# p of images 2 to 7 with three nested products and two reads by ScalarE, f by seven products for images 7 and 8, bias in column tiles

## The chip, the cores and the metric

The kernel runs on one core of one Trainium2 chip. The metric is the device time of one execution in microseconds. The engines are TensorE (PE, with its weight loads PEld), VectorE (DVE), ScalarE (ACT), GpSimd (POOL), and SyncE (SP), which issues most DMAs. All data are fp32.

## The reference, cut to what matters

The input x has 8 images of 512 channels and 32 x 32 = 1024 positions. Two layers follow each other:

```
q, k, v = Wq x + bq, Wk x + bk, Wv x + bv           # 8 heads of 64 channels
attn    = softmax(q^T k / 8)                        # per head, 1024 x 1024
x       = x + Wp (attn v) + bp                      # "p"
g, theta, phi = g_w x + g_b, theta_w x + theta_b, phi_w x + phi_b   # 256 channels each
f       = theta phi^T / 1024                        # 256 x 256
z       = W_w (f g) + W_b + x
out     = batch norm of z over images and positions
```

So every 1x1 convolution is a product of a weight matrix of 512 (or 256) x 512 with a matrix of 512 x 1024 per image. f is a product over the 1024 positions.

## The kernel before, in words

**Stages.** Images are counted 1 to 8 here, b = 0 to 7 in the code. For each image the kernel runs attention, then q, v and k of the next image, then p of this image (`project`), then theta and phi together (tensor ptp into tp, `theta_phi`), then f, g and the product of f with W_w (`nonlocal_`). TensorE works through one strict queue. A helper `pe` (and `dve` for some operations of VectorE and GpSimd) pins operations in the order of the program; where an operation isn't pinned, a scheduler places it. SP issues the loads of weights in the order of the program; a load waits until its buffer (a ring of four) is free.

**Products by seven.** A product of matrices cut into 2 x 2 blocks is done by seven products of half size in place of eight, with sums of blocks on both sides (`weight_sums`, `data_sums`/`more_sums`: t1 to t4 of the data). The table `SEVEN` lists them: name, weight block, data block, slot, and which quarters of the result the product goes to. A half-size product of p is four matmuls of 128x512. `nested` does the same again inside a half-size product: seven quarter-size products, each one matmul of 128x256, in place of four matmuls of 128x512. It needs inner sums of the weight block (`nest`, made once and kept in DRAM) and of the data block (`inner_sums`).

**The stage p.** For images 2 to 7 `seven` takes its products from `INNER["p"]`: five plain products (`FIVE`) and two nested ones. The third entry of `INNER["p"]`, read by `for _ in range(next(counts, 0)): next(steps)`, says how many nested steps follow each main matmul: none for the first four, then one after each. The results lie in PSUM in four slots of two banks each; tags[0] and tags[1] hold slots 0 and 1 of the main products, tags[2:] the nested ones. Main products in order: "11" (slot 0), s1t1 (slot 1), s2t2 (slot 0), s4 (slot 1), s3t3 (slot 0). After each product its result is added into quarters of x by VectorE: the first time with the bias bp (L773, two 128x512 operations), later by one 128x1024 operation (L471). The sums t1 and t2 of the new x, for the next stage, come after p; t3 and t4 in the next stage (L261).

**Before p.** In the stage k of the next image GpSimd makes the sums of o, the attention's output (`i_o` and `t_o`), and, at the end of `six`, two 128x1024 additions into k (`add("22", "T7")`, `add("21", "T7")`).

**f.** `make_f` is 16 matmuls of 128x256 and one copy by ScalarE; `seven_f` is 28 matmuls of 128x128 with sums on VectorE before (`f_sums`) and after. Images 1 to 6 use `seven_f`, images 7 and 8 `make_f`. f of image 7 is computed inside the attention of image 8 (`held_f`, at its step 2), f of image 8 within pg of its own `nonlocal_`.

**The bias.** At image 1 only, four products of one column (`bias_product`) add Wp bv to bp: TensorE into PSUM, a copy by ScalarE, an addition by VectorE, ahead of the products den that give the softmax denominators.

Of the kernel before, what the change touches and what calls it, by code (L numbers as in the profile page):

```python
# [8 lines left out]
F32 = mybir.dt.float32  # L9
# [7 lines left out]
P = 128  # L17
# [13 lines left out]
def unshifted(ctx: ExitStack, tc: tile.TileContext, a: dict, out: bass.AP):  # L31
# [79 lines left out]
    for b in range(1, B):  # L111
# [4 lines left out]
    PAIRS = ((1, 6), (3, 4), (5, 2))  # L116
    UNITS = {"WqT": PAIRS, "WkT": PAIRS, "WvT": PAIRS, "WpT": ((1, 2), (3, 4, 5), (6,)), "tp": ((1, 2), (3, 4, 5), (6,)),
             "WgT": (range(7),)}
# [41 lines left out]
    def fetch(w, n, t=None, dma=None):  # L160
        dma, name = dma or nc.sync, w.name
        if t is None:
            t = wf0.tile([P, 2 * w.half], F32, tag="w0", name=f"w0_{name}") if n == "first" else \
                wr.tile([P, WIDTH], F32, tag="w", name=f"w_{name}_{n}")
        blocks = w.place(n, t)
        if name in kept:
            of = kept["plain" if w.last else name][n]
            sp(dma.dma_start(w.whole(n) if w.last else w.tiles[n], of))
            return
        if n == 0:  # L170
            corner[name] = block(f"a21_{name}")[:, :, :w.half]
# [36 lines left out]
    def inner_weights(w, i):  # L208
# [3 lines left out]
                for to, l, r, op in ((s3, a11, a21, ALU.subtract), (a21, a21, a22, ALU.add), (s2, a21, a11, ALU.subtract),  # L212
                                     (s4, a12, s2, ALU.subtract))]

    def nest(w, i):
        for one in inner_weights(w, i):
            one()
# [10 lines left out]
    def join_bias(t):  # L228
# [6 lines left out]
        def more(c):  # L235
# [4 lines left out]
                15: more(1), 17: get(2, 1), 22: more(2), 25: get(3, 1), 30: more(3)}  # L240

    def bias_product(t, ps):
        for oc in range(CC):
            pe(nc.tensor.matmul(ps[:, oc:oc + 1], t[:, oc * P:(oc + 1) * P], ones, start=True, stop=True,
                                skip_group_check=True))
# [30 lines left out]
    def quarters_of(t):  # L276
# [50 lines left out]
    def seven(name, w, data, positions_out, first, add, between=None, early=False,  # L327
              by_chunk=False, inner=None):

# [19 lines left out]
        for n, (what, wi, di, s, reads) in enumerate(products):  # L349
# [14 lines left out]
            for i, (to_ps, at, lhsT, rhs, k) in enumerate(work):  # L364
# [11 lines left out]

    def six(name, w, data, positions_out, at, begin, third, fills, by_scalar=False):

# [78 lines left out]
        if by_scalar:  # L457
            add("T7", "T6")
        add("22", "T7")
        add("21", "T7")  # L460

# [40 lines left out]

    ones = const.tile([P, 1], F32, tag="ones", name="ones")
    nc.vector.memset(ones, 1.0)
    eps = const.tile([P, 1], F32, tag="eps", name="eps")
# [22 lines left out]
    def heads_of(b, what, w, bias, data, pin=lambda ins: None, steps=None, fills=None, **how):  # L528
# [3 lines left out]
        if fills is not None:  # L532
            def begin(to, ps, i):
                nc.scalar.activation(to, ps, AF.Identity, bias=bias[:, i:i + 1])
# [7 lines left out]
            six(f"p{what}_{b}", w, data, False, lambda q: t[:, rows(q), cols(q)], begin, third, fills,  # L542
                what == "q")
            return t
# [31 lines left out]
    def attention(b, q, k, v, near_end, make_f=None):  # L576
# [10 lines left out]
        rows = {}  # L587
        tags = list(free)

        def part(u):  # L590
# [92 lines left out]
        def all_denominators(ps):  # L683

            t = folded.pop("t")
            if b == 0:
                bias_product(t[:, 3, :], ps[:, 1, :CC])
            den = ps[:, 0, :256]
            in_tiles(den, [(folds4, t[:, 0, :])])
            ri = t[:, 2, :256]  # L690
            dve(nc.vector.reciprocal(ri, den))
# [73 lines left out]

    def project(b, xt, w, between, data):
        def first(q, ps):
            if isinstance(q[0], slice):
                ps = ps.unsqueeze(1)
            for m in range(ps.shape[1]):  # L770
# [3 lines left out]
                if b == B - 1 and q in ("11", "22"):  # L774
                    dve(ins)

        seven(f"pp_{b}", w, data, False, first, add_to(xt), between, early=b == B - 1 and "later",
              inner="p" if 0 < b < B - 1 else None)

# [87 lines left out]

    def make_f(b, tp, ps):
        f = block("f").rearrange("p a n -> p (a n)")[:, :IC * CI].rearrange("p (c d) -> p c d", c=IC)
        ps = ps[:, 0, :].rearrange("p (c d) -> p c d", c=IC)  # L870
        order = [*range(NB // 2, NB), *range(NB // 2)]
        for c in range(IC):
            for i in order:
                pe(nc.tensor.matmul(ps[:, c, :], tp[:, i, c * P:(c + 1) * P], tp[:, i, CI:],
                                    start=(i == order[0]), stop=(i == order[-1])))
        nc.scalar.mul(f, ps, 1.0 / N)
        return f

    def nonlocal_(b, xt, data, f, wg, before_wf, between=None, theta=None, tp=None):

        scaled = theta is None
        if theta:
            phi = f_sums(b, tp, CI)
            f = lambda ps: seven_f(theta, phi, ps)
        ww = block(f"ww_{b}")
# [10 lines left out]
        def first(q, ps):  # L896
# [3 lines left out]
            else:  # L900
# [3 lines left out]
              lambda q, ps: nc.vector.tensor_tensor(part(q), part(q), ps[:, 0, :], ALU.add),  # L904
              between or {4 if theta else 5: f_meanwhile}, early=bool(between))
        f = fs[0]
# [3 lines left out]
        for d in range(IC):  # L910
            ps = next_bank(f"pwf_{b}_{d}")[:, 0, :]
            for c in range(IC):
                pe(nc.tensor.matmul(ps, f[:, c, d * P:(d + 1) * P], ww[:, c, :], start=(c == 0), stop=(c == IC - 1)))  # L913
            nc.scalar.mul(wf[:, d, :], ps, 1.0 if scaled else 1.0 / N)
        if b >= B - LATE:
# [151 lines left out]
    for b in range(B):  # L1067
        last = b == B - 1
        nxt = {}
        if b == 1:  # L1070
            nest(w_tp, 1)
            nest(w_tp, 2)
            keep("tp", w_tp, (0,))
            load_w()
# [34 lines left out]
        def held_f(ps):  # L1109
            held["f"] = make_f(b - 1, held["tp"], ps)  # L1110

        o, denominators, normalize = attention(b, q, k, v, near_end, held_f if last else None)
        between = None
        if not last:
# [4 lines left out]
                (0, 0): t4[:1], (0, 3): t4[1:2], (0, 13): t4[2:3], (1, 0): t4[3:]})  # L1119
            products = normalize(denominators(next_bank(f"den_{b}")))  # L1120
            v = values(b + 1, weights("WvT"), data, fills={(1, 13): products})

# [4 lines left out]
            if b:  # L1127
                more = [lambda: inner_sums(nxt["o"], "t4", dve, nc.gpsimd)]
                o_sums = [lambda: inner_sums(nxt["o"], "21", dve, nc.gpsimd), *o_sums]
            else:  # L1130
                w_p = loaded[1]
                more = [lambda i=i: weight_sums(w_p, corner["WpT"], (i,), dve, nc.gpsimd) for i in (3, 4, 5)]
            k = heads_of(b + 1, "k", weights("WkT"), bk, data, dve, steps=dk, fills={
                (0, 13): [*o_sums, *(more if b else ())], (1, 13): () if b else more,
                (2, 0): () if b else [lambda: weight_sums(w_p, corner["WpT"], (6,), dve, nc.gpsimd)]})
        else:
# [17 lines left out]
        w = weights("WpT", sums_done=True)  # L1154
        project(b, xt, w, between, nxt["o"])
        if b == 0:
# [9 lines left out]
        data = data_sums(quarters_of(xt), f"x1_{b}", (1, 2, 3, 4) if last else (1, 2))  # L1166
        if last:
            reload_chunks(B - LATE)
        elif b > B - LATE and b != B - 2:
            z[b] = [xt[:, cc, :] for cc in range(CC)]  # L1170
# [25 lines left out]
        def before_wf():  # L1196
            if last:
# [3 lines left out]
                take_back(B - LATE + 1)  # L1201

        if last:
            take_back(B - LATE)
        if b == B - 2:
            held.update(x=xt, tp=tp)
        else:
            nonlocal_(b, xt, data, lambda ps: make_f(b, tp, ps), weights("WgT"), before_wf,
                      theta=of_theta[0] if of_theta else None, tp=tp)
            load_w()  # L1210
# [230 lines left out]
```

## Time and profile before

| What | us |
|---|---|
| Median of 3 runs (2103.86 to 2104.8) | 2104.62 |
| The profiled execution | 2104.33 |
| Its span | 2102.5 |
| Mean granted TensorE clock, share of full | 0.996 |

Groups of instructions that the change concerns (busy time in all and mean of one, then the idle time of the engine before them):

```profile
L365 PE MATMUL pp<-t_o,w_WpT 128*128 128x512 f32 x208 | 101.0, 592 | 0.0
L365 PE MATMUL pp<-o,w_WpT 128*128 128x512 f32 x144 | 67.7, 592 | 0.0
L773 DVE SCALAR_TENSOR_TENSOR x<-pp,bp,x 128x512 f32<-128x512 f32 x52 | 37.5, 746 | 33.0 <-PE pp L365 33.0
```

A matmul of the program on fp32 data appears as two records, so 208 and 144 records of pp stand for 176 matmuls (20 each for images 2 to 7, 28 each for images 1 and 8). The busy time of matmuls counts overlapping records once, while the mean of one includes the time until its result is written. In the timeline, a row merges neighbouring instructions of one kind: its start, its length, engine, line, operation, and how many; the bracket tells how long the engine was idle before and what ended that.

### The profile page before, as it was taken

The page shows a single profiled execution, that of the slowest core. Times are in us where ns is not written, and L with a number is a line of the kernel's source. Part 1 is how long each engine was busy: PE and PEld are TensorE (multiplying, and loading weights), DVE is VectorE, ACT ScalarE, POOL GpSimd, SP SyncE. Part 2 cuts the span into 40 slices and gives each one's busy share as a digit, 9 for nine tenths or more (in the row PEclk, how much of TensorE's full clock was granted, in tenths as well). Part 3 has the DMA queues.
Part 4 walks back from the last instruction along what each step waited for, and adds up shares of the span by engine and source line. Part 5 has one row for each costly group of instructions (what it writes and reads, how often), then busy time and mean ns, then how long its engine had stood idle before and what let it go on. Part 6 is the DMA issues. An engine that isn't in the chain of part 4 may idle for free.

```text
span 2102.5 us, 34141 instructions
## 1 busy us (share of the span) xinstructions
PE 2080.0 (99%) x13598; PEld 1170.5 (56%) x13598; DVE 1426.5 (68%) x2137; ACT 790.5 (38%) x1045; POOL 734.0 (35%) x637
## 2 busy tenths in 40 slices
PE   9999999999999999999999999999999999999995
PEld 4535864358733677336773377633875348733472
DVE  5587567875677656876567766677665775656746
ACT  1465204652046410464105631066312653056116
POOL 0024800348113581134812356123670338411010
PEclk9999999999999999999999999999999999999998
DMA  6254534345343443435324363153644345312768
GB/s 230 83 145 77 162 137 142 42 87 153 105 115 38 94 142 106 118 40 115 131 90 122 40 147 119 67 126 41 159 144 154 40 53 168 100 29 39 218 253 321
DMA packets 76727, 246.78 MB, mean 117 GB/s; under 512 B 16657, under 2 KB 25105, under 8 KB 74513
## 3 DMA queue, kind: packets, MB, share of 16 engines
q1 hardware_dynamic: 62688, 218.16, 31.8%
q0 software_dynamic: 12016, 24.80, 12.2%
q8 instruction: 109, 1.79, 0.4%
q10 hardware_dynamic: 1856, 1.56, 0.3%
q14 instruction: 58, 0.47, 0.1%
HBM read 163.20 MB, written 47.71 MB: 100 GB/s over the span
## 4 chain that ended last, share of the span: by engine, by line
PE 98%; ACT 1%; DVE 1%; DMA 0%; issue 0%; DVEq 0%
PE ps L602 21%; PE po L628 21%; PE pp L365 7%; PE ptp L365 7%; PE pv_in L441 6%; PE pk_in L444 6%; PE pq_in L444 6%; PE pg L365 5%; PE pz L365 3%; PE ptp_in_s L313 2%; PE pf L857 2%; PE pp_in_s L316 2%; PE pwf L913 1%; PE pv L408 1%; PE pq L411 1%; PE pq L365 1%
## 5 line engine op out<-in xcount | busy, mean ns | idle before, releaser
L605 ACT ACTIVATE e<-ps 128x1024 f32<-128x1024 f32 x512 | 523.0, 1025 | 422.2 <-PE ps L602 412.1
L658 POOL DMA_DIRECT2D fold<-acc x336 | 257.1, 816 | 949.2 <-DMA fold<-acc 637.4
L611 DVE TENSOR_TENSOR acc<-acc,e 128x1024 f32<-128x1024 f32 x384 | 469.9, 1224 | 103.1 <-ACT e L605 93.6
L602 PE MATMUL ps<-q,k 64*64 64x512 f32 x4096 | 529.4, 589 | 0.0
L628 PE MATMUL po<-e,v 64*64 64x512 f32 x4096 | 528.7, 589 | 0.0
L628 PEld LDWEIGHTS po<-e,v 64*64 64x64 f32 x4096 | 156.6, 133 | 282.9 <-issue 275.7
L602 PEld LDWEIGHTS ps<-q,k 64*64 64x64 f32 x4096 | 155.5, 133 | 283.4 <-issue 275.6
L901 ACT ACTIVATE g<-pg,gb 128x512 f32<-128x512 f32 x31 | 21.3, 688 | 436.3 <-PE pg L365 436.2
L609 DVE TENSOR_TENSOR acc<-e,e 128x1024 f32<-128x1024 f32 x64 | 78.3, 1224 | 118.2 <-ACT e L605 116.0
L365 PE MATMUL pp<-t_o,w_WpT 128*128 128x512 f32 x208 | 101.0, 592 | 0.0
L365 PE MATMUL ptp<-w_tp,t_x 128*128 128x256 f32 x400 | 96.1, 379 | 0.0
L720 POOL TENSOR_TENSOR o<-o,r 128x1024 f32<-128x1024 f32 x28 | 65.5, 2362 | 36.3 <-DMA r<-den_d 35.8
L365 PEld LDWEIGHTS ptp<-w_tp,t_x 128*128 128x128 f32 x400 | 72.3, 190 | 7.8
L452 DVE TENSOR_TENSOR k<-k,pk_in 128x256 f32<-128x256 f32 x112 | 46.8, 421 | 39.5 <-PE pk_in L444 35.0
L365 PE MATMUL ptp<-w_tp,x 128*128 128x256 f32 x272 | 69.6, 380 | 0.0
L365 PE MATMUL pp<-o,w_WpT 128*128 128x512 f32 x144 | 67.7, 592 | 0.0
L450 ACT COPY v<-pv_in 128x256 f32<-128x256 f32 x84 | 31.4, 374 | 95.8 <-DVE T_pv L452 25.5
L452 DVE TENSOR_TENSOR v<-v,pv_in 128x256 f32<-128x256 f32 x112 | 46.2, 421 | 29.6 <-PE pv_in L441 23.1
L450 ACT COPY k<-pk_in 128x256 f32<-128x256 f32 x84 | 31.3, 372 | 91.6 <-PE pk_in L444 89.9
L773 DVE SCALAR_TENSOR_TENSOR x<-pp,bp,x 128x512 f32<-128x512 f32 x52 | 37.5, 746 | 33.0 <-PE pp L365 33.0
L441 PE MATMUL pv_in<-w_WvT,i_t_x 128*128 128x128 f32 x448 | 59.2, 275 | 0.0
L444 PE MATMUL pk_in<-i_t_x,w_WkT 128*128 128x256 f32 x224 | 57.8, 381 | 0.0
(249 smaller groups left out, 3149.5 us busy)
## 6 DMA issues: line engine op xcount, KB each, us to landing
fold<-acc POOLq DMA_DIRECT2D x336, 64.0 KB, 3.0
w_WqT<-kept_WqT SPq DMA_DIRECT2D x21, 896.0 KB, 5.8
w_WvT<-kept_WvT SPq DMA_DIRECT2D x21, 896.0 KB, 5.5
w_WkT<-kept_WkT SPq DMA_DIRECT2D x21, 896.0 KB, 6.7
r<-den_d SPq DMA_DIRECT2D x32, 512.0 KB, 7.0
x<-in_x_dram SPq DMA_DIRECT2D x30, 512.0 KB, 6.1
spill<-x SPq DMA_DIRECT2D x24, 512.0 KB, 4.0
z<-spill SPq DMA_DIRECT2D x24, 512.0 KB, 8.8
```

The costliest lines, as they stand in the source:

```text
L365: pe(nc.tensor.matmul(to_ps, lhsT(k), rhs(k), start=(s, at) not in begun, stop=(k == nk - 1), skip_group_check=True))
L441: pe(nc.tensor.matmul(ps[:, i, :], d[:, i * P:(i + 1) * P], a, start=start and not i, stop=True, skip_group_check=True))
L444: pe(nc.tensor.matmul(ps, a, d, start=start, stop=True, skip_group_check=True))
L450: nc.scalar.copy(piece(q, i, j), ps)
L452: dve(nc.vector.tensor_tensor(piece(q, i, j), piece(q, i, j), ps, ALU.add))
L602: pe(nc.tensor.matmul(ps[c * P // 2:(c + 1) * P // 2, j, :], k[r, p, keys], q[r, p, h * 512:(h + 1) * 512], start=True, stop=True, skip_gr ...
L605: nc.scalar.activation(e, ps, AF.Exp, scale=SCALE)
L609: nc.vector.tensor_tensor(accs[u], es[u, 0], e, ALU.add)
L611: ins = nc.vector.tensor_tensor(accs[u], accs[u], e, ALU.add)
L628: pe(nc.tensor.matmul(ps[j * D:(j + 1) * D, r, :], v[keys, m, (2 * p + j) * D:(2 * p + j + 1) * D], e[keys, j, :], start=(m == 0), stop=(m ...
L658: nc.gpsimd.dma_start(to, of, accum_op=ALU.add)
L720: dve((engine or nc.vector).tensor_tensor(at, at, of, ALU.mult))
```

## The change

It has six parts.

1. p of images 2 to 7: `INNER["p"]` takes four plain products and three nested ones. The product s4 is no longer plain; its block (weights 6, data "22", into quarter "12") is the third nested one. The counts of nested steps become [1] * 10 + [2, 1] + [2] * 4.
2. s1t1 and s2t2 of p are read by ScalarE (with bias where there is one destination, else a copy) into a buffer, and GpSimd adds that to x (`by_scalar`). The two last additions into k move from the end of k's stage behind GpSimd's addition for s2t2 (`later`). t1 of the new x comes before the reads of the last product (`ahead_of_last`).
3. The inner sums of o's quarter "22" are made by GpSimd in k's stage.
4. Weights of p: the units are (1, 2), (3, 4), (5, 6). The last comes by two loads, the plain block 5 and the block 6 with its inner sums, which `nest_apart` makes once at image 2 and stores. At image 1 the block sums 5 and 6 are made by VectorE before p.
5. The bias product is four matmuls of 32x128 in column tiles, behind den. Its row is copied by ScalarE, turned by two DMAs through DRAM (`turn_bias`), and added to bp in k's stage.
6. f of images 7 and 8 is computed by `seven_f`; `make_f` goes away. In the attention of image 8 it stands at step 6 in place of 2, in pg of image 8 after product 4 in place of 5. The scaling by 1/1024 is always in the copy of wf. For image 8 the loads of four chunks of z (`reload_chunks`) are issued after tp in place of after p.

```diff
-    UNITS = {..., "WpT": ((1, 2), (3, 4, 5), (6,)), "tp": ((1, 2), (3, 4, 5), (6,)),
+    UNITS = {..., "WpT": ((1, 2), (3, 4), (5, 6)), "tp": ((1, 2), (3, 4, 5), (6,)),
...
-            sp(dma.dma_start(w.whole(n) if w.last else w.tiles[n], of))
+            if n == 2 and name == "WpT" and not w.last:
+                sp(dma.dma_start(w[5], of[:, 0, :].rearrange("p (k f) -> p k f", k=2)))
+                sp(dma.dma_start(w.tiles[n][:, WIDTH // 2:], kept["block 6"]))
+            else:
+                sp(dma.dma_start(w.whole(n) if len(of.shape) == 3 else w.tiles[n], of))
...
+    def nest_apart(w, n, i):
+        t = w3.tile([P, N], F32, tag="acc", name="apart")[:, :WIDTH // 2]
+        to = t[:, :2 * w.half]
+        sp(nc.sync.dma_start(to, kept["plain"][n][:, 1, :]))
+        w.at[i] = to.rearrange("p (k f) -> p k f", k=2)
+        w.extra[i] = t[:, 2 * w.half:].rearrange("p (i f) -> p i f", i=3)
+        nest(w, i)
+        kept[f"block {i}"] = dram.tile([P, WIDTH // 2], F32, tag=f"block{i}", name=f"block{i}")
+        sp(nc.sync.dma_start(kept[f"block {i}"], t))
...
     def bias_product(t, ps):
+        of = P // CC
         for oc in range(CC):
-            pe(nc.tensor.matmul(ps[:, oc:oc + 1], t[:, oc * P:(oc + 1) * P], ones, start=True, stop=True,
+            pe(nc.tensor.matmul(ps[oc * of:(oc + 1) * of, :], alike, t[:, oc * P:(oc + 1) * P], start=True, stop=True,
                                 skip_group_check=True))
-        got = small.tile([P, CC], F32, tag="got", name="got")
-        nc.scalar.copy(got, ps)
-        nc.vector.tensor_tensor(bp, bp, got, ALU.add)
+        nc.scalar.copy(row, ps)
+
+    def turn_bias():
+        d = dram.tile([CC, P], F32, tag="bias", name="bias_d")
+        sp(nc.sync.dma_start(d, row.rearrange("(c s) n -> c s n", c=CC)[:, 0, :]))
+        sp(nc.sync.dma_start(got, d.rearrange("c p -> p c")))
...
-    INNER = {"p": (FIVE, ((1, "21", "11", False), (2, "t4", "21", True)), [0] * 4 + [1] * 14),
+    FOUR = (SEVEN[0], ("s1t1", 3, "t1", 1, (("22", False), ("12", False))), ("s2t2", 4, "t2", 0, (("12", True),)),
+            ("s3t3", 5, "t3", 0, (("22", True), ("21", False))))
+
+    INNER = {"p": (FOUR, ((6, "22", "12", False), (1, "21", "11", False), (2, "t4", "21", True)),
+                   [1] * 10 + [2, 1] + [2] * 4),
...
-            read(reads, ps)
+            if inner and ahead_of_last and n == len(products) - 1:
+                ahead_of_last()
+            if inner and what in via:
+                via[what](reads, ps)
+            else:
+                read(reads, ps)
...
-        add("22", "T7")
-        add("21", "T7")
+        ends = [lambda q=q: add(q, "T7") for q in ("22", "21")]
+        if later is not None:
+            later += ends
+            return
+        for one in ends:
+            one()
...
+        def by_scalar(reads, ps):
+            t = block(f"read_{b}")
+            for m in range(2):
+                if len(reads) == 1:
+                    nc.scalar.activation(t[:, m, :], ps[:, m, :], AF.Identity, bias=bp[:, m:m + 1])
+                else:
+                    nc.scalar.copy(t[:, m, :], ps[:, m, :])
+            for q, _ in reads:
+                at = xt[:, rows(q), cols(q)]
+                dve(nc.gpsimd.tensor_tensor(at, at, t, ALU.add))
+            if len(reads) == 1:
+                for one in later:
+                    one()
...
         tags = list(free)
+        if make_f:
+            tags[2:] = tags[:1:-1]
...
-            if make_f and i == 2:
-                make_f(bank(tags[2], f"pf_{b - 1}"))
+            if make_f and i == 6:
+                make_f(bank(tags[3], f"pf_{b - 1}"))
...
-            held["f"] = make_f(b - 1, held["tp"], ps)
+            held["f"] = seven_f(*held["both"], ps)
...
-                o_sums = [lambda: inner_sums(nxt["o"], "21", dve, nc.gpsimd), *o_sums]
+                o_sums = [*(lambda of=of: inner_sums(nxt["o"], of, dve, nc.gpsimd) for of in ("22", "21")), *o_sums]
...
-        between = {} if last else {4 if b else 5: lambda: b < B - 2 and of_theta.append(f_sums(b, tps[0], 0))}
+        between = {4 if b else 5: lambda: of_theta.append(f_sums(b, tps[0], 0))}
...
+        both = of_theta[0], f_sums(b, tp, CI)
         if last:
+            reload_chunks(B - LATE)
             take_back(B - LATE)
```

More of the change, by code (lines that the diff above doesn't have):

```diff
@@ L116, in unshifted @@
     PAIRS = ((1, 6), (3, 4), (5, 2))
-    UNITS = {"WqT": PAIRS, "WkT": PAIRS, "WvT": PAIRS, "WpT": ((1, 2), (3, 4, 5), (6,)), "tp": ((1, 2), (3, 4, 5), (6,)),
+    UNITS = {"WqT": PAIRS, "WkT": PAIRS, "WvT": PAIRS, "WpT": ((1, 2), (3, 4), (5, 6)), "tp": ((1, 2), (3, 4, 5), (6,)),
              "WgT": (range(7),)}
@@ L240, in join_bias @@
                 15: more(1), 17: get(2, 1), 22: more(2), 25: get(3, 1), 30: more(3)}
+    row, got = (const.tile([P, n], F32, tag=f"bias{n}", name=f"bias{n}") for n in (P, CC))
     def bias_product(t, ps):
+        of = P // CC
         for oc in range(CC):
-            pe(nc.tensor.matmul(ps[:, oc:oc + 1], t[:, oc * P:(oc + 1) * P], ones, start=True, stop=True,
+            pe(nc.tensor.matmul(ps[oc * of:(oc + 1) * of, :], alike, t[:, oc * P:(oc + 1) * P], start=True, stop=True,
                                 skip_group_check=True))
-        got = small.tile([P, CC], F32, tag="got", name="got")
-        nc.scalar.copy(got, ps)
-        nc.vector.tensor_tensor(bp, bp, got, ALU.add)
+        nc.scalar.copy(row, ps)
[3 more added lines that the diff above has]
+        sp(nc.sync.dma_start(got, d.rearrange("c p -> p c")))
     def data_sums(quarters, name, which=(1, 2, 3, 4), **how):
@@ L327, in seven @@
     def seven(name, w, data, positions_out, first, add, between=None, early=False,
-              by_chunk=False, inner=None):
+              by_chunk=False, inner=None, via=(), ahead_of_last=None):
         nk, half = w.shape[2], w.shape[3]
@@ L375, in unshifted, with six @@
     ORDER = "0a 0b 1a 2a 2b 1b 5a 4a 5b 4b 3a 3b 6a 6b".split()
-    def six(name, w, data, positions_out, at, begin, third, fills, by_scalar=False):
+    def six(name, w, data, positions_out, at, begin, third, fills, by_scalar=False, later=None):
         fills = dict(fills)
@@ L501, in unshifted @@
     fetch(wv, 0)
-    ones = const.tile([P, 1], F32, tag="ones", name="ones")
-    nc.vector.memset(ones, 1.0)
+    alike = const.tile([P, P // CC], F32, tag="ones", name="alike")
+    nc.vector.memset(alike, 1.0)
+    ones = alike[:, :1]
     eps = const.tile([P, 1], F32, tag="eps", name="eps")
@@ L542, in heads_of @@
             six(f"p{what}_{b}", w, data, False, lambda q: t[:, rows(q), cols(q)], begin, third, fills,
-                what == "q")
+                what == "q", how.get("later"))
             return t
@@ L685, in all_denominators @@
             t = folded.pop("t")
-            if b == 0:
-                bias_product(t[:, 3, :], ps[:, 1, :CC])
             den = ps[:, 0, :256]
             in_tiles(den, [(folds4, t[:, 0, :])])
+            if b == 0:
+                bias_product(t[:, 3, :], ps[:, 1, :P])
             ri = t[:, 2, :256]
@@ L764, in attention, with project @@
         return o["o"], all_denominators, normalize
-    def project(b, xt, w, between, data):
+    def project(b, xt, w, between, data, x1, later=()):
         def first(q, ps):
@@ L775, in first @@
                     dve(ins)
+        def by_scalar(reads, ps):
[11 more added lines that the diff above has]
+                    one()
         seven(f"pp_{b}", w, data, False, first, add_to(xt), between, early=b == B - 1 and "later",
-              inner="p" if 0 < b < B - 1 else None)
+              inner="p" if 0 < b < B - 1 else None,
+              via={"s1t1": by_scalar, "s2t2": by_scalar}, ahead_of_last=lambda: more_sums(x1, (1,), dve))
     tps = []
@@ L866, in seven_f, with nonlocal_ @@
         return f
[L868 to L884, printed above, removed]
+    def nonlocal_(b, xt, data, f, wg, before_wf, between=None, sums=None):
+        if sums:
+            f = lambda ps: seven_f(*sums, ps)
         ww = block(f"ww_{b}")
@@ L904, in nonlocal_ @@
               lambda q, ps: nc.vector.tensor_tensor(part(q), part(q), ps[:, 0, :], ALU.add),
-              between or {4 if theta else 5: f_meanwhile}, early=bool(between))
+              between or {4: f_meanwhile}, early=bool(between))
         f = fs[0]
@@ L913, in nonlocal_ @@
                 pe(nc.tensor.matmul(ps, f[:, c, d * P:(d + 1) * P], ww[:, c, :], start=(c == 0), stop=(c == IC - 1)))
-            nc.scalar.mul(wf[:, d, :], ps, 1.0 if scaled else 1.0 / N)
+            nc.scalar.mul(wf[:, d, :], ps, 1.0 / N)
         if b >= B - LATE:
@@ L1070, in unshifted @@
         if b == 1:
+            nest_apart(Weights("WpT"), 2, 6)
             nest(w_tp, 1)
@@ L1120, in unshifted @@
             products = normalize(denominators(next_bank(f"den_{b}")))
+            if b == 0:
+                turn_bias()
             v = values(b + 1, weights("WvT"), data, fills={(1, 13): products})
@@ L1128, in unshifted @@
                 more = [lambda: inner_sums(nxt["o"], "t4", dve, nc.gpsimd)]
-                o_sums = [lambda: inner_sums(nxt["o"], "21", dve, nc.gpsimd), *o_sums]
+                o_sums = [*(lambda of=of: inner_sums(nxt["o"], of, dve, nc.gpsimd) for of in ("22", "21")), *o_sums]
             else:
                 w_p = loaded[1]
-                more = [lambda i=i: weight_sums(w_p, corner["WpT"], (i,), dve, nc.gpsimd) for i in (3, 4, 5)]
-            k = heads_of(b + 1, "k", weights("WkT"), bk, data, dve, steps=dk, fills={
+                more = [lambda i=i: weight_sums(w_p, corner["WpT"], (i,), dve, nc.gpsimd) for i in (3, 4)]
+            later = [] if b else None
+            k = heads_of(b + 1, "k", weights("WkT"), bk, data, dve, steps=dk, later=later, fills={
                 (0, 13): [*o_sums, *(more if b else ())], (1, 13): () if b else more,
-                (2, 0): () if b else [lambda: weight_sums(w_p, corner["WpT"], (6,), dve, nc.gpsimd)]})
+                (2, 0): () if b else [lambda: dve(nc.vector.tensor_tensor(bp, bp, got, ALU.add))]})
+            if b == 0:
+                weight_sums(w_p, corner["WpT"], (5, 6), dve)
         else:
@@ L1154, in unshifted @@
         w = weights("WpT", sums_done=True)
-        project(b, xt, w, between, nxt["o"])
+        x1 = data_sums(quarters_of(xt), f"x1_{b}", ())
+        project(b, xt, w, between, nxt["o"], x1, later if 0 < b < B - 1 else ())
         if b == 0:
@@ L1165, in unshifted @@
                 nc.sync.dma_start(spill[b][:, cc, :], xt[:, cc, :])
[L1166 to L1170, printed above, removed]
+        data = x1
+        if 0 < b < B - 1:
+            more_sums(data, (2,), dve)
+        else:
+            more_sums(data, (1, 2, 3, 4) if last else (1, 2))
         of_theta = []
         w = weights("tp")
-        between = {} if last else {4 if b else 5: lambda: b < B - 2 and of_theta.append(f_sums(b, tps[0], 0))}
+        between = {4 if b else 5: lambda: of_theta.append(f_sums(b, tps[0], 0))}
         if b == 0:
@@ L1201, in before_wf @@
                 take_back(B - LATE + 1)
+        both = of_theta[0], f_sums(b, tp, CI)
         if last:
+            reload_chunks(B - LATE)
             take_back(B - LATE)
         if b == B - 2:
-            held.update(x=xt, tp=tp)
+            held.update(x=xt, both=both)
         else:
-            nonlocal_(b, xt, data, lambda ps: make_f(b, tp, ps), weights("WgT"), before_wf,
-                      theta=of_theta[0] if of_theta else None, tp=tp)
+            nonlocal_(b, xt, data, None, weights("WgT"), before_wf, sums=both)
             load_w()
```

## The prediction

> **What bounds the kernel now.** I read, in this order, the busy shares, the chain that ended last, TensorE's waits, and the timelines of the stages that the change touches. The page first:
>
> ```profile
> span 2102.5 us, 34141 instructions
> PE 2080.0 (99%) x13598; PEld 1170.5 (56%) x13598; DVE 1426.5 (68%) x2137; ACT 790.5 (38%) x1045; POOL 734.0 (35%) x637
> ...
> PE 98%; ACT 1%; DVE 1%; DMA 0%; issue 0%; DVEq 0%
> ```
>
> The list of waits of TensorE (time in all, times, longest) is three lines long:
>
> ```profile
> PE count L1227 <- DVE good L1225: 8.6, 1, 8.6
> PE warm_ps L494 <- DVE four L515: 1.1, 1, 1.1
> PE den L680 <- issue: 0.3, 1, 0.3
> ```
>
> Two of these lie outside the images' stages, one is the bias at image 1. So in the stages TensorE is never late: work taken from it is worth its whole time, work given to other engines is free, and a wait that appears on TensorE costs its whole length. The change does all three.
>
> **The stage p, image 2.** The timeline gives the ends, the pieces of the chain the pace between them (start, us, engine, tile, records):
>
> ```profile
> 514.09 3.60 PE L365 MATMUL pp<-o,w_WpT 128*128 128x512 f32 x8
> 517.52 1.02 PE L365 MATMUL pp<-t_o,w_WpT 128*128 128x512 f32 x2
> 518.38 0.59 PE L316 MATMUL pp_in_s<-o,w_WpT 128*128 128x256 f32 x2
> ...
> 518.54 0.43 PE pp_in_s L316 x2
> 518.97 0.86 PE pp L365 x2
> ```
>
> One matmul of the program is two records. A 128x512 one takes 0.8585 us of TensorE (four take 517.52 - 514.09 = 3.43), a 128x256 one 0.431. The first ptp starts at 537.30, so p takes 23.21 us, and 20 x 0.8585 + 14 x 0.431 = 23.20: the stage is the plain sum of its matmuls. A record's duration (0.59 for 512 columns) is 0.163 longer than its share of the pace, 0.429: that is latency, paid only where somebody waits for the end.
>
> How reads follow, in the timelines of VectorE and ScalarE:
>
> ```profile
> 522.45 0.75 DVE L773 SCALAR_TENSOR_TENSOR x<-pp,bp,x 128x512 f32<-128x512 f32 x1 [0.44 <-PE pp L365]
> 523.12 0.41 DVE L471 TENSOR_TENSOR x<-x,pp_in_s 128x256 f32<-128x256 f32 x1
> 523.45 0.74 DVE L773 SCALAR_TENSOR_TENSOR x<-pp,bp,x 128x512 f32<-128x512 f32 x1
> ...
> 494.29 0.69 ACT L534 ACTIVATE T_pk<-pk,bk 128x512 f32<-128x512 f32 x1 [1.41 <-PE pk L411]
> 494.88 0.68 ACT L534 ACTIVATE k<-pk,bk 128x512 f32<-128x512 f32 x1
> ```
>
> The reader is to see that the first half of s1t1 is read only at 522.45, when the eighth main matmul has ended, not when its own half was done: a product's read waits for the whole product. And two ScalarE reads of 128x512 in a row take 0.59 + 0.68 = 1.27 us.
>
> **What the Trainium skill says.** "PSUM — Partial Sum Buffer", section "PSUM bank collisions raise a hardware error", has it that two engines must not touch one bank and quadrant at once, so a matmul into a bank has to wait for the read out of it; the trace before shows no such wait, because a product in the other slot always lies between. In the same page's "The four PSUM rules" GpSimd has no access to PSUM, which is why ScalarE has to copy before GpSimd can add. "ScalarE: Activation LUTs", section "What ACT_TABLE_LOAD costs", prices an ACTIVATE with a pointer bias at about 280 ns + 0.833 ns a column, 0.71 us for 512, with about 0.09 overlap back to back; the trace has 0.69 and an overlap of 0.10. I use the trace's.
>
> **Part 1, p of images 2 to 7 (six times).** Product s4 leaves: 4 x 0.8585 = 3.43. A third nested product comes: 7 x 0.431 = 3.02. That is -0.42 an image, -2.5 in all.
>
> **Part 2, the wait that this makes.** s4 used slot 1 and stood between s2t2 and s3t3, both in slot 0. Without it s3t3's first matmul (the 13th main one) follows s2t2's last (the 12th) with one nested step between (the count list reads 2, 1, then 2). In the built program that 13th matmul waits for ScalarE's second read of s2t2, and the read waits for the 12th. Let the 12th start at 0. It ends at 0.429 + 0.592 = 1.02; ScalarE starts 0.04 later (as VectorE does above); the pair ends at 1.06 + 0.59 + 0.68 = 2.33. TensorE restarts about 0.155 after an end of a ScalarE copy (a q copy ends at 452.774, the gated matmul runs at 453.146, of which 0.216 is the matmul before it), so at 2.48. Without the wait it would start at 0.8585 + 0.431 = 1.29. The stall is 1.19 us. The queue runs in order, so the nested steps behind it stand too; nothing covers it. Bounds: 0.9 (TensorE restarts at once, reads at their shortest) to 1.5 (a start 0.15 later on each side). Six times 1.19 is +7.1 (5.4 to 9.0). ScalarE itself is free: it has no work between the k copy at 514.29 and 562.9.
>
> **Part 3, what the other engines do in p.** VectorE loses four reads of 0.75 and one of 1.22 us and gains seven nested reads of 0.42 to 0.48; GpSimd gains three 128x1024 adds (2.36 us each) and keeps the two k adds, later, in a gap of 14.7 us in which it waits today (t_x at L261). Four more GpSimd sums of 128x256 (0.72 each) go before o's sums, of which the last is ready at 517.0 today and has slack. One place is tight: tp's third product needs tp's first read off VectorE, now behind the last p read, an x sum of 1.22 and t1 and t2. I make it ready about 6.4 us after p's end against a need at 6.9: a margin of 0.45. Cost nothing; without that cover, what exceeds it, six times.
>
> **Part 4, weights.** The unit (5, 6) comes in two loads, block 6 with its sums made once through a scratch tile at image 2. SP's loads of this size land in 2.6 to 4.3 us; block 6 is asked for at about 508, needed at 514.9. The tp units are released 1 to 3 us differently and needed 3 us and more after they land. On SP the extra issues of 0.3 us stand before loads with slack. At image 1 two sums of blocks move from GpSimd to VectorE ahead of p, whose first product needs neither. Nothing, bounds 0 to +1 once.
>
> **Part 5, the bias at image 1.** Today TensorE and a wait for ScalarE and VectorE stand in the way:
>
> ```profile
> 209.45 0.95 PE L244 MATMUL den<-ones,fold 128*128 128x1 f32 x8
> 210.70 0.64 PE L680 MATMUL den<-fold,folds 128*32 128x256 f32 x8 [0.30 <-issue]
> 211.27 1.99 PE L408 MATMUL pv<-w_WvT,x 128*128 128x256 f32 x8
> ...
> 469.43 0.64 PE L680 MATMUL den<-fold,folds 128*32 128x256 f32 x8
> 470.00 1.35 PE L408 MATMUL pv<-w_WvT,x 128*128 128x256 f32 x5
> ```
>
> From the first of these to pv is 1.82 us at image 1, 0.57 at image 2: the bias costs 1.25. After, it is four column tiles of 32x128. The den tiles of the same form need 0.57 for 256 columns, where eight records of 0.2155 in a row would need 1.72: they run side by side, so 128 columns cost about 0.3. Then ScalarE's row and the two DMAs are waited for by no matmul before p. -0.9; bounds -0.3 (tiles in a row, 0.9 us) to -1.2.
>
> **Part 6, f of images 7 and 8.** Plain f takes 7.11 us (1837.25 to 1844.36) and 6.90 (2031.06 to 2037.96); f by seven products takes 6.25 at image 2 (569.45 to 575.70). -0.85 and -0.65, -1.5 together; I take -1.4. The sixteen sums for it on VectorE (0.6 each) and the eight joins lie beside attention and pg; the four phi sums of image 7 end near 1842.8, the first product of f at step 6 comes after about 1844. A lateness there would cost up to 1 us once.
>
> **Sum.** -2.5 + 7.1 - 0.9 - 1.4 = +2.3, against the profiled execution's 2104.33 (span 2102.5 and 1.8 around it): 2106.6. The median of the runs is 2104.62, 0.29 above it, so 2106.8.
>
> **The rivals.** A difference of 0.2% (4.2 us) is about what a measurement of this kernel tells from no change.
> (A) As summed, the read of s2t2 stalls TensorE 0.9 to 1.5 an image: 2105.2 to 2108.8. For it: the two products are neighbours in one slot and the read alone is longer than the one nested step. Against it: none of these waits is in the trace before. Chance 0.60.
> (B) The stall is shorter because the first half is freed earlier, 0.5 an image: 2106.8 - 6 x 0.69 = 2102.7. Against it: today's reads wait for whole products. Chance 0.08.
> (C) The stall doesn't show: -2.5 - 0.9 - 1.4 = -4.8, 2099.8. For it: the ends of matmuls in the trace are modelled, and a wait of the built program need not end last. Against it: one nested step of 0.43 us can't hide 1.27 us of reads. Chance 0.12.
> (D) Slower: VectorE at the seam of p and tp becomes the bound. t1, the last x add, t2 and tp's first read are four operations of 1.22 us in a row, and three of them now share the time with GpSimd's moved adds (one sum in the trace, at 545.5, took 1.31 beside GpSimd). It decides once VectorE is more than 0.45 us late; 1.1 us late gives 6 x 0.65 = +3.9: 2110.7. Chance 0.20.
>
> **How the numbers follow.** The likeliest is A, 2106.8, whose own range is 2105.2 to 2108.8. From 2101.0 to 2110.5 leaves out C and the half of D. Faster by over 0.2%: C and little else, 0.13. Slower by over 0.2%: D and A's edge, 0.21. Within 0.2%: 0.66.
>
> **What would show it.** In the profile after, TensorE's waits should list pp with ScalarE's read of pp as the releaser, six times about 1.2 us; p of image 2 should take 22.8 + 1.2 = 24.0 us instead of 23.2; f at images 7 and 8 6.25 us; from den to pv at image 1 about 0.9. If p takes 22.8, C holds; if waits of ptp on VectorE's tp read appear, D. A wait of pp on a weight load or of pp_in_s on GpSimd would make Part 3 or 4 wrong.

## The result, and the profile after

The kernel after takes 2108.30 us in the median of 20 runs (2107.18 to 2109.27), beside 2104.59 for the kernel before in 20 runs (2103.81 to 2105.67). The ratio is 1.0017, 95% interval 1.0011 to 1.0024: 3.7 us slower, where 2.2 slower was forecast and the likeliest case ran from 2105.2 to 2108.8. The profiled execution has a span of 2106.1 us, 3.6 more than before, at the same clock of 0.996.

The shares of busy time after:

```profile
PE 2077.6 (99%) x13682; PEld 1176.4 (56%) x13682; DVE 1440.6 (68%) x2193; ACT 803.3 (38%) x1067; POOL 791.8 (38%) x677
```

TensorE is 2.4 us less busy and yet ends later. The list of its waits (engine and line, what ended the wait, time in all, times, longest) says where (its two other lines lie outside the images' stages and are as long as before):

```profile
...
PE pp L390 <- issue: 5.8, 6, 1.0
...
```

den's wait is gone and pp's has come, six times, once for each of images 2 to 7. The list names no releaser ("issue"): in the trace the wait stands ahead of the matmul's weight load, which starts at 530.68. The timelines of TensorE, ScalarE and GpSimd around that place in image 2 show what ended it (start, us, engine, line, operation, records; the first row of TensorE is the start of p, the last the start of tp):

```profile
513.66 1.02 PE L390 MATMUL pp<-o,w_WpT 128*128 128x512 f32 x2
...
528.29 1.02 PE L390 MATMUL pp<-t_o,w_WpT 128*128 128x512 f32 x2
529.14 0.59 PE L341 MATMUL pp_in_s<-o,w_WpT 128*128 128x256 f32 x2
530.71 1.10 PE L390 MATMUL pp<-t_o,w_WpT 128*128 128x512 f32 x2 [0.97 <-issue]
531.64 0.59 PE L341 MATMUL pp_in_s<-i_o,w_WpT 128*128 128x256 f32 x2
...
537.67 3.62 PE L390 MATMUL ptp<-w_tp,x 128*128 128x256 f32 x16
...
529.35 1.27 ACT L818 ACTIVATE read<-pp,bp 128x512 f32<-128x512 f32 x2 [4.52 <-PE pp L390]
...
530.75 2.35 POOL L823 TENSOR_TENSOR x<-x,read 128x1024 f32<-128x1024 f32 x1 [1.18 <-ACT read L818]
```

The reader is to see the chain step by step. s2t2's last matmul starts at 528.29 and ends at 529.31; ScalarE starts at 529.35 and ends at 530.62; the next main matmul starts at 530.71, and its pair takes 0.93 us to the next record in place of 0.86. The nested step in between covers only 529.14 to 529.57. In pace, s3t3's first matmul ends 2.07 us after that nested step, where 0.86 would do: a stall of 1.21 us. The whole stage lasts from 513.66 to 537.67, 24.01 us. GpSimd's addition isn't what is waited for: it starts at 530.75, after the matmul.

By stages, from the starts of the first matmuls in both timelines (us; a stage ends where the next begins):

| stage | before | after | difference |
|---|---|---|---|
| first q | 24.65 | 24.98 | +0.33 |
| den and bias to pv, image 1 | 1.81 | 0.79 | -1.02 |
| p, each of images 2 to 7 | 23.21 | 24.01 | +0.80 |
| tp after it, image 2 | 23.57 | 23.57 | 0 |
| attention of image 8 to den, with f of image 7 | 86.39 | 85.76 | -0.63 |
| pg and f of image 8 | 18.93 | 18.27 | -0.66 |
| last matmul (`count`) to the end of the span | 12.8 | 13.1 | +0.3 |

The rest, 0.46 us, is q of image 2 (+0.1), q of image 3 and k of image 8 (+0.18 each). At the last two the weight load that comes late is released by a read by VectorE (L482).

### The profile page after: what moved, and what is told of

Same layout as the page of the kernel before. It is cut to its first block, busy times and chain, and to the rows that moved or that the text cites. A ratio compares the mean times of both kernels' runs of the same rounds, so it can differ in the third digit from the quotient of the medians.

```text
span 2106.1 us, 34471 instructions
## 1 busy us (share of the span) xinstructions
PE 2077.6 (99%) x13682; PEld 1176.4 (56%) x13682; DVE 1440.6 (68%) x2193; ACT 803.3 (38%) x1067; POOL 791.8 (38%) x677
## 4 chain that ended last, share of the span: by engine, by line
PE 97%; ACT 1%; DVE 1%; issue 0%; DMA 0%; DVEq 0%
PE ps L639 21%; PE po L665 21%; PE ptp L390 7%; PE pp L390 6%; PE pv_in L471 6%; PE pk_in L474 6%; PE pq_in L474 6%; PE pg L390 5%; PE pz L390 3%; PE pp_in_s L341 3%; PE pf L909 2%; PE ptp_in_s L338 2%; PE pwf L952 1%; PE pv L438 1%; PE pq L441 1%; PE pq L390 1%
## 5 line engine op out<-in xcount | busy, mean ns | idle before, releaser
L505 DVE TENSOR_TENSOR x<-x,pp_in_s 128x256 f32<-128x256 f32 x102 | 42.9, 420 | 71.7 <-PE pp_in_s L341 71.6
L482 DVE TENSOR_TENSOR k<-k,pk_in 128x256 f32<-128x256 f32 x112 | 46.8, 421 | 39.5 <-PE pk_in L474 35.4
L482 DVE TENSOR_TENSOR v<-v,pv_in 128x256 f32<-128x256 f32 x112 | 46.3, 422 | 29.3 <-PE pv_in L471 22.8
L474 PE MATMUL pq_in<-i_t_x,w_WqT 128*128 128x256 f32 x224 | 57.5, 379 | 0.0
```

Of the source, the lines that this page charges most:

```text
L474: pe(nc.tensor.matmul(ps, a, d, start=start, stop=True, skip_group_check=True))
L482: dve(nc.vector.tensor_tensor(piece(q, i, j), piece(q, i, j), ps, ALU.add))
```

## The experiments

**One step, none or four between the two products.** The theory (theory 1 in the expectations) is the one of the prediction: the stall is ScalarE's read of s2t2, as far as nested steps don't cover it. The rival is that p became dearer for another reason. The number of nested steps in p stays 21; only their places change. cover0:

```diff
-                   [1] * 10 + [2, 1] + [2] * 4),
+                   [1] * 9 + [2] * 2 + [0] + [2] * 4),
```

> No nested step between the two products. Theory 1: the stall grows by one step, to 1.64 us, p takes 24.45, the time is 2108.3 + 6 x 0.43 = 2110.9. Rival: 2108.

Measured: 2110.56 us, ratio to before 1.0030 (1.0018 to 1.0041), and p takes 24.44 us at all six images. The list of waits:

```profile
PE pp L390 <- issue: 8.4, 6, 1.4
```

One step less costs 0.43 us of stall an image, its own length: nothing but these steps covers the read. That speaks for the theory. The other direction, cover3 and cover4:

```diff
-                   [1] * 10 + [2, 1] + [2] * 4),
+                   [0] * 2 + [1] * 8 + [2, 3] + [2] * 4),     # cover3
+                   [0] * 2 + [1] * 9 + [4] + [2] * 4),        # cover4
```

> Three nested steps between the two products. Theory 1: a stall of 1.21 - 0.86 = 0.35 us an image stays, p takes 23.15, the time is 2108.3 - 6 x 0.86 = 2103.1. Rival: 2108.

> Four nested steps (1.72 us) stand between s2t2's last matmul and s3t3's first, in place of one; the number of steps in p stays 21. Theory 1 (the stall is ScalarE's read of s2t2, covered by 0.43 us of its 1.62): the list of TensorE's waits loses pp, p of image 2 takes 22.8 us, and the time is 2108.3 - 6 x 1.21 = 2101.0. Rival (the stage lost time by dearer nested steps or by GpSimd, whatever stands in the gap): p stays at 24.0 and the time at 2108. A third way: four steps in a row outrun VectorE, which reads each of them, and pp_in_s waits in place of pp: p between 23 and 24.

Measured: 2123.68 (1.0090, 1.0074 to 1.0107) and 2124.8 (1.0097, 1.0080 to 1.0114). Both expectations missed by 20 us and more, on the wrong side. The wait of pp is gone, but another has come in its place. Waits of TensorE in cover4, then the timelines of TensorE, VectorE and GpSimd at image 2:

```profile
PE pp_in_s L341 <- DVE x L505: 15.2, 6, 2.7
...
529.66 0.70 PE L341 MATMUL pp_in_s<-i_o,w_WpT 128*128 128x256 f32 x2 [2.53 <-DVE x L505]
...
529.19 0.75 DVE L505 TENSOR_TENSOR x<-x,pp_in_s 128x256 f32<-128x256 f32 x2 [5.04 <-POOL x L823]
...
524.51 4.64 POOL L823 TENSOR_TENSOR x<-x,read 128x1024 f32<-128x1024 f32 x2
```

GpSimd adds s1t1 into quarters 22 and 12 of x from 524.51 to 529.15. The first nested product also goes to quarter 12. By starting the steps two matmuls later, its last reads fell behind s1t1 in the program, and so behind GpSimd's 4.6 us; VectorE's queue stood for 5.04 us, the slots of the nested steps stayed full, and TensorE waited 2.5 us. p of image 2 takes 26.04 us here, the other five 25.97 to 27.77. So these two runs moved more than the cover, and the next two take the steps from other places.

**The cover alone.**

```diff
-                   [1] * 10 + [2, 1] + [2] * 4),
+                   [1] * 9 + [0, 1, 3] + [2] * 4),            # late3
+                   [1] * 9 + [0, 0, 4] + [2] * 4),            # late4
```

> The same with three steps between the two products. Theory 1: a stall of 1.21 - 0.86 = 0.35 us an image, p 23.15, 2103.1. Rival: as for four steps, 2103.5 or more.

> Again four nested steps between s2t2 and s3t3, but taken from the places behind the ninth and later main matmuls, so that the first nested product (quarter 12, which GpSimd adds to as well) has had all its seven steps before s1t1 ends, as in the kernel after. Theory 1 with the reading of cover4 (there a nested read into quarter 12 stood behind GpSimd's 4.7 us of additions for s1t1): pp and pp_in_s both leave the list of TensorE's waits, p of image 2 takes 22.8 us, the time is 2108.3 - 6 x 1.21 = 2101.0. Rival (four steps in a row outrun VectorE): pp_in_s still waits, p at 23.2 or more, 2103.5 or more.

Measured: late3 2102.82 (ratio to before 0.9991, 0.9983 to 1.0000), late4 2103.45 (0.9995, 0.9986 to 1.0003). Both are 4.9 to 5.5 us faster than the kernel after, with nothing changed but the places of two or three steps. p takes 23.15 us in late3, as expected to the hundredth, and 23.24 in late4, where 22.8 was expected. TensorE in late4 around the four steps:

```profile
527.99 0.59 PE L341 MATMUL pp_in_s<-i_o,w_WpT 128*128 128x256 f32 x2
528.42 0.59 PE L341 MATMUL pp_in_s<-o,w_WpT 128*128 128x256 f32 x2
529.09 0.70 PE L341 MATMUL pp_in_s<-i_o,w_WpT 128*128 128x256 f32 x2
529.63 0.69 PE L341 MATMUL pp_in_s<-o,w_WpT 128*128 128x256 f32 x2
530.15 1.02 PE L390 MATMUL pp<-t_o,w_WpT 128*128 128x512 f32 x2
```

A step takes 0.43 us; here they follow each other after 0.43, 0.67, 0.54 and 0.52. The nested steps share two slots. The third one would be due at 528.85, but VectorE reads the result of the first from 528.62 to 529.04. That is the rival of late4, worth 0.44 us an image against the plain sum of the matmuls, 22.80. Four steps cover ScalarE's read and pay it back among themselves; three leave 0.35 of it.

**Who reads.**

```diff
-              via={"s1t1": by_scalar, "s2t2": by_scalar}, ahead_of_last=...)
+              via={"s1t1": by_scalar}, ahead_of_last=...)
...
-            if len(reads) == 1:
+            if len(reads) == 2:
                 for one in later:
```

> s2t2 is read and added by VectorE (two operations of 0.75 us, as in the kernel before) in place of ScalarE and GpSimd; the rest as in the kernel after. Theory 1 (the two products are neighbours in one slot, whoever reads): the wait of pp stays and names VectorE, 1.2 to 1.6 us an image, the time is 2108 to 2111. Rival (ScalarE's reads are the cause): the wait goes, 2101.

The second part of the edit lets the additions into k follow GpSimd's addition for s1t1, since there is none for s2t2 any more.

Measured: 2111.96 (1.0038, 1.0023 to 1.0052), pp waits 10.2 us in all, up to 1.7 at a time, p takes 24.73 us. The stall doesn't go away with ScalarE; it grows to 1.94 us, more than the 1.2 to 1.6 expected, and the list says "issue" here too. VectorE at image 2:

```profile
529.11 0.75 DVE L810 SCALAR_TENSOR_TENSOR x<-pp,bp,x 128x512 f32<-128x512 f32 x1 [0.69 <-POOL x L823]
529.78 0.41 DVE L505 TENSOR_TENSOR x<-x,pp_in_s 128x256 f32<-128x256 f32 x1
530.11 0.75 DVE L810 SCALAR_TENSOR_TENSOR x<-pp,bp,x 128x512 f32<-128x512 f32 x1
```

So the neighbourhood of the two products in one slot is the cause, whoever reads. The next main matmul starts at 530.95, 0.09 us after VectorE's second read ends. Of the two readers ScalarE is the better: VectorE waits for GpSimd's addition into the same quarter first, and has a nested read between its two.

**A main product in between.** s3t3 adds to what s2t2 left in slot 0, so it can't move to slot 1. What can move is half of s1t1, which is in slot 1:

```diff
-            ("s1t1", 3, "t1", 1, (("22", False), ("12", False))), ("s2t2", 4, "t2", 0, (("12", True),)),
+            ("s1t1", 3, "t1", 1, (), 0), ("s2t2", 4, "t2", 0, (("12", True),)),
+            ("s1t1", 3, "t1", 1, (("22", False), ("12", False)), 1),
...
-                   [1] * 10 + [2, 1] + [2] * 4),
+                   [1] * 11 + [2] * 5),
```

> The kernel after with s1t1's second half (two matmuls of 128x512 in slot 1) moved between s2t2 and s3t3, in place of nested steps; GpSimd adds s2t2 first, then s1t1, then into k. Two matmuls and two or more nested steps, 2.6 us, now lie where 1.62 are needed, and no more than two nested steps stand in a row. Theory 1: p of image 2 takes 22.8 us, no wait of pp or pp_in_s, 2108.3 - 6 x 1.21 = 2101.0. Rival (ScalarE and GpSimd can't keep up with two reads close together, and the seam to tp waits): p 22.8 but ptp longer than 23.57, 2102 or more.

Measured: 2108.44 (1.0019, 1.0011 to 1.0027), no gain on the kernel after. p takes 22.80 us, just what the sum of its matmuls gives; but tp, right after it, takes 24.85 in place of 23.57. Waits of TensorE, then VectorE and GpSimd at the seam from p to tp of image 2:

```profile
PE ptp L390 <- PE ptp L390: 2.7, 6, 0.5
PE ptp L390 <- DVE tp L862: 1.9, 6, 0.3
...
538.44 3.16 DVE L282 TENSOR_TENSOR t_x<-x 128x1024 f32<-128x1024 f32 x1
...
535.86 4.66 POOL L428 TENSOR_TENSOR k<-k,T_pk 128x1024 f32<-128x1024 f32 x2
```

The same two places in the kernel after:

```profile
538.47 1.22 DVE L282 TENSOR_TENSOR t_x<-x 128x1024 f32<-128x1024 f32 x1
...
533.06 4.67 POOL L426 TENSOR_TENSOR k<-k,T_pk 128x1024 f32<-128x1024 f32 x2
```

There the sum t1 takes 1.22 us, and GpSimd has ended its additions into k at 537.73, before t1 starts at 538.47. Here GpSimd starts later, since ScalarE's first read comes 3.8 us later, and is in its second addition until 540.5 when t1 comes. t1 then takes 3.16 us: it ends at 541.60, 1.08 us after GpSimd's addition, nearly its own length. The two work on different tensors, x and k, so t1 doesn't wait for a result of GpSimd's addition. Everything behind it on VectorE is 1.9 us late, and tp's third product with it. This is the prediction's rival D, brought about by GpSimd's end, not by the load of VectorE.

**The bias and f alone**, put on the kernel before (parts 5 and 6 of the change, each by itself, then both):

> The kernel before with part 6 alone (f of images 7 and 8 by seven products). From the trace after (6.45 and 6.25 us in place of 7.10 and 6.91): 2104.6 - 1.3 = 2103.3. Rival: VectorE's extra sums delay the last attention, nothing is gained, 2104.6.

> The kernel before with part 5 alone (the bias in column tiles). Theory: 2104.6 - 0.9 = 2103.7. In the trace after, the first q stage took 0.33 us longer than before; if the bias part's constants cause that, this run shows a first q of 24.98 us in place of 24.65 and gains only 0.6, 2104.0; if not, it shows 24.65.

> The kernel before with parts 5 and 6: 2104.6 - 1.3 - 0.9 = 2102.4, if they add.

Measured: f alone 2103.19 (0.9992, 0.9984 to 1.0001), 1.5 us below before; the bias alone 2104.28 (0.9998, 0.9989 to 1.0006), 0.4 below; both 2102.60 (0.9991, 0.9984 to 0.9997), 2.1 below. The two add up, and they are the parts of the change that gain; each alone has an interval that includes no change. The bias in column tiles saves 1.02 us between q and pv in the profile of bias_only too (0.79 in place of 1.81), but that profile gives it back elsewhere: the first q is 0.5 us longer, q of image 2 0.09 and k of image 8 0.35. The last two are in the profile of f_and_bias as well, and in none without the bias part.

> The kernel before unchanged, to see how far its profile repeats: the first q stage at 24.65 us, p of image 2 at 23.2, and the end of the span after the last count, 2102.5 - 2089.7 = 12.8 us. If the first q or the end vary by 0.3 us, what the trace after shows there is no effect of the change.

Measured: a span of 2102.6, the first q 24.68, p of image 2 23.21, 12.8 us after the last count. The first q lies at 24.65, 24.68 and 24.71 in the three profiles without the bias part, and from 24.40 to 25.31 in the eleven with it, on both sides of before: 25.17 in bias_only and 24.68 in f_and_bias, for instance. So the +0.33 of the table is no fixed cost of one part. Record by record (after, bias_only, late3 and cover3 beside before), the differences lie mostly among its first ten records of matmuls, and in after, bias_only and cover3 the trace names the first loads of Wq there. What sets them was not found, and whether the kernels with the bias part repeat as well as before does was not measured.

**Where the bias is added.** The addition of the turned bias into bp, 128x4 on VectorE, has no fixed length. It stands in the stage k behind the attention of image 1, which the expectations call k of image 1; what is computed there is k of image 2. Two profiles, after and late3, each with GpSimd beside it:

```profile
249.76 0.78 DVE L1178 TENSOR_TENSOR bp<-bp,bias 128x4 f32<-128x4 f32 x1
248.17 2.35 POOL L282 TENSOR_TENSOR t_o<-o,t_o 128x1024 f32<-128x1024 f32 x1
...
250.09 1.91 DVE L1178 TENSOR_TENSOR bp<-bp,bias 128x4 f32<-128x4 f32 x1
249.64 2.35 POOL L282 TENSOR_TENSOR t_o<-o,t_o 128x1024 f32<-128x1024 f32 x1
```

In both it ends with GpSimd's operation, at 250.54 beside 250.52, and at 252.00 beside 251.99. In late3 this k is 0.93 us longer (22.71 in place of 21.78), in cover3 1.24, in cover4 and split 0.88, in late4 0.11; in after, cover0 and dve_reads it isn't longer. So the last run moved it in the kernel of the split:

```diff
-                (2, 0): () if b else [lambda: dve(nc.vector.tensor_tensor(bp, bp, got, ALU.add))]})
+                (2, 0): ()})
             if b == 0:
                 weight_sums(w_p, corner["WpT"], (5, 6), dve)
+                dve(nc.vector.tensor_tensor(bp, bp, got, ALU.add))
```

> split, and the addition of the bias into bp (128x4 on VectorE, which took 0.25 to 2.2 us in the runs, each time ending with the GpSimd operation beside it, and made k of image 1 up to 1.2 us longer) moved behind the sums of p's weights after k. Theory: k of image 1 stays at 21.78 us in every profile, the time is that of split less 0 to 0.9, about 2100.6. Rival: the addition delays those sums or p's first read instead, no gain.

Measured: 2109.40 (1.0024, 1.0014 to 1.0035); the 2100.6 rested on the gain that split didn't bring. This k is back at 21.77, but p of image 1 grows from 24.03 to 26.13. The rival holds: three operations of VectorE in a row now stand beside GpSimd's additions into k, each ends 0.02 to 0.55 us after one of these, and p's first read is behind. TensorE's list of waits has 1.9 us of pp for VectorE's read (L812). The three:

```profile
254.96 2.05 DVE L107 TENSOR_TENSOR w_WpT<-w_WpT,a_WpT 128x512 f32<-128x512 f32 x1
256.93 2.83 DVE L107 TENSOR_TENSOR w_WpT<-w_WpT,w_WpT 128x512 f32<-128x512 f32 x1
259.69 2.30 DVE L1183 TENSOR_TENSOR bp<-bp,bias 128x4 f32<-128x4 f32 x1
```

**What is the best.** late3 (2102.82) and the kernel before with parts 5 and 6 alone (2102.60) lie together, 1.8 and 2.1 us below before, too close to be told apart. Both beat before and after in the medians; only the second's interval is clear of 1. With the three-step cover, p gains 0.06 us an image, so the third nested product gains little more than its stall costs. Two things were not tried. One is a split p with the additions into k put elsewhere, which might keep p at 22.80 and t1 free of GpSimd. The other is a wait by halves: s3t3's first matmul writes the half of the slot that ScalarE read first, and that read ended at 530.03, 0.58 us before the second, so a program in which this matmul waits for the first read alone might save up to 0.58 us an image (an estimate from the trace after).

## Why the prediction was right

**Part 1 and 2, p.** The sum gave 24.0 us for p and a stall of 1.19; the trace has 24.01 and 1.21, at each of the six images, and p moved by 0.43 us a step with none and with three steps between the products, as the working says (with four, VectorE's reads of the steps themselves came in). ScalarE's start (0.04 after the last matmul's end) and the restart (0.09 to the matmul and 0.07 in its first pair, 0.16 in all) are those of the estimate. Rival B, a shorter stall because the first half is freed earlier, is out: the matmul starts 0.09 us after the end of the second read, though the first had ended 0.58 before that. Rival C, no stall, is out by the 1.21. One detail was off: it was foretold that the list of waits would name ScalarE, and it doesn't; one has to go to the timelines.

**Part 3.** The seam to tp held: tp of image 2 takes 23.57 as before. But that was luck as far as the working goes, for its margin left out what decides it. It counted VectorE's own operations, and took from one sum of 1.31 us that working beside GpSimd costs little; that sum had begun at 545.55, 0.23 us before GpSimd's short operation ended. split shows that GpSimd's end is what counts, and the room there was 0.74 us (537.73 to 538.47). Rival D was about rightly priced: by its rule that lateness beyond 0.45 us is paid, the 1.9 us of split would cost 1.45 an image, and 1.28 were paid. But its cause was another.

**Part 4.** No wait for a weight load or for GpSimd's sums appears in p. Nothing was the right cost. The 0.18 us at q of image 3 and k of image 8 don't belong here: VectorE's reads stand before them, not loads, and in bias_only, which has none of this part, k of image 8 is 0.35 us longer.

**Part 5, the bias.** -0.9 forecast, -1.02 in the stage, -0.4 in the median of the run alone, with an interval that includes no change. The side costs were not in the sum: the two later stages named above, and an addition on VectorE that waits for GpSimd and now can hold k's chain. Before, the same addition took 0.26 us at a place where GpSimd's operation was ending. That it cost nothing in the profile after was luck: with the same code it cost 0.88 to 1.24 us in four other kernels.

**Part 6, f.** -1.4 forecast; -1.29 in the trace, -1.47 in the run alone. Image 7's f takes 6.45 us inside attention and not 6.25.

**What the sum lacked**, 1.3 us of span: the first q (+0.33), q of image 2 (+0.1), two stalls of 0.18 in q of image 3 and k of image 8, and 0.3 us after the last matmul make 1.1; the rest is p, 4.8 us in six images where 4.6 were summed. The 0.3 us are in the profiles of all kernels with the new p (13.1 us) and in none of the others (12.7 to 12.8); why was not found out. None of them touches the mechanism, and with them the forecast of +2.2 became +3.7 in the medians (+3.6 in the span).

## What to carry to other kernels

When a product is taken out of a chain of products, look at what it kept apart: its neighbours may share an accumulator, and the read between them, latency and all, then stands bare on TensorE. Work that is moved into such a gap has its own order: before moving it, follow which region it writes and which slow engine is queued on the same region. In this kernel a sum on VectorE with both inputs in SBUF waited for as much as a whole GpSimd operation, so ask where GpSimd will be before planning one that somebody waits for.

## What the runs showed that was not expected

In these profiles a VectorE operation with both inputs in SBUF that starts while a GpSimd sum runs stands until that sum has ended. A 128x4 addition took 0.25 to 2.3 us, a 128x512 one up to 2.83 in place of 0.69, a 128x1024 one 3.16 in place of 1.22; they ended 0.02, 0.55 and 1.08 us after GpSimd's sum. It goes the other way too: in the profile after, a GpSimd sum of 128x256 that started at 546.00, 0.08 us after a sum of VectorE, took 1.72 us in place of 0.73. Operations of VectorE that read PSUM kept their lengths: of 487 additions of 128x256 from PSUM that started beside a GpSimd sum in the profile after, the longest took 0.43 us, and the median of 0.42 is that of the others.
